# The attention of layer L2: where the softmax is divided by its sums

## Chip, cores and metric

The kernel runs on one core of one Trainium2 chip. The metric is the device time of one execution in microseconds (us); several runs of the same kernel are made, and the median is compared. A profile of one execution says what every engine did and when. The engines are PE (TensorE, matrix products and transposes), DVE (VectorE), ACT (ScalarE), POOL (GpSimd) and SP (which issues transfers). Each works through its own queue in order; they wait for one another by semaphores.

## What is computed

The reference is a network of four layers, each with an attention between two feed-forward halves, on 8 sequences of 512 tokens with 128 features. The change touches the attention of the layer called L2: 16 heads of width 64, causal, with a bias that grows linearly with the distance of the tokens.

```
q, k, v = (x @ Wq), (x @ Wk), (x @ Wv)        # each reshaped to (b, n, 16, 64)
bias    = slope[:, None, None] * (pos[:, None] - pos[None, :])
scores  = einsum('bihd,bjhd->bhij', q, k) * 64 ** -0.5 + bias[None]
scores  = where(pos[:, None] >= pos[None, :], scores, -1e30)
attn    = softmax(scores, axis=-1)
out     = einsum('bhij,bjhd->bihd', attn, v).reshape(b, n, 16 * 64)
return out @ Wo + bo
```

A softmax divides the exponentials of a row by their sum. The division can stand anywhere between the exponential and the end of the product with `v`, since the sum is one number for each head and each query.

## The kernel before

The attention is in `l2_block`. It works in steps `n` = 0 to 63: sequence `b = n // 8`, and in it a pair of heads, so eight steps make a batch (one sequence). A few steps at either end only fill and empty the pipeline. In each step the loop at L1660 writes the work of three neighbouring pairs interleaved:

- `score(n, i)` multiplies the queries of token tile `i` (128 tokens) with all keys up to it (128, 256, 384 or 512 columns), on PE (L1553). One DVE instruction adds the bias and takes the smallest element of each row (L1557), and leaves an ACT exponential to be issued (L1560), which also writes the sums of the rows to `sums[n]`. Signs are turned, so the smallest is what is taken off. Tiles 2 and 1 of pair `n` are scored in step `n`; tiles 3 and 0 already at the end of the step before. The exponentials lie in `es[n]`, 128 x 1280 for each of the two heads.
- `turn(n - 1, m)`, m = 0 to 4, transposes the 128x128 blocks of exponentials of the pair before (L1579, PE), so that keys lie along the partitions; ACT copies each group of four from PSUM (L1581).
- `invert(n - 2)` takes the reciprocals of the sums (L1586, DVE) and spreads each over 64 columns (`rb`, L1588, DVE).
- `weigh(n - 2)` multiplies the turned exponentials with the values into the PSUM tile `o` (L1602, PE). Features lie along its partitions, tokens along its columns. To divide it by the sums, these must be turned too: four transposes of `rb` go to `rp` (L1607, PE), ACT copies `rp` to `rt` (L1609), and DVE multiplies `o` by `rt` into `atts[b]` (L1610).
- `project(n + 1)` makes queries and keys of the next pair (L1522, copied by ACT at L1524), `values(n)` the values of two pairs in every second step (L1535, copied by DVE at L1536), and `leave(b)` once a batch the product with `Wo` (L1616) and the addition to `x` (L1618, DVE).

Between these, three times a step, `works` issues pieces of other layers' work: the feed-forward halves before and after, for sequences that are ready. Their places are written as numbers (`self.plan`): three units to a step. Lines that are named below: L170 statistics for the normalisation and L200 its application on POOL (`whiten`), L310 the products of the last layer's experts (PE's part is L308), L271 and L274 the feed-forward half of L2, L322 to L359 the routing, L906 to L1013 the feed-forward half of L1. The order of PE, ACT and DVE in this stage is that in which the code issues (`manual_schedule`); POOL's and SP's are the scheduler's.

[...] The tile `s` of the scores takes two banks, twice; all else, `tp`, `pp`, `vp`, `o`, `rp`, `op`, `pt`, `yp`, shares four under the tag `mm`. A product can only start when a bank has been read out.

## Time and profile before

| what | value |
|---|---|
| median of 3 runs | 2802.72 us (2797.55 to 2804.87) |
| the profiled execution | 2823.91 us, its span 2822.0 us |
| PE, DVE, ACT, POOL busy | 2508.1, 1886.6, 1741.5, 1177.3 us |
| stage of L2's attention, from its first products to its last | 1143.4 to about 2050 us |
| in it PE, DVE, ACT, POOL busy | 872, 559, 594, 328 us |

The profile comes as a page (busy times, the span in 40 slices, DMA queues, the chain of work that ended last, the costliest groups of instructions) and as a trace that answers questions: what an engine did in a stretch, who waited for whom, what the chain went through. The groups of the lines that the change touches, for the stretch from 1143 to 2052 us (line, engine, operation, tiles, shapes, count | busy us, mean ns | idle time before them):

```profile
L1607 PE MATMUL rp<-cst,rb 128*128 128x128 f32 x256 | 42.0, 286 | 0.2 <-DVE rb L1588 0.2
L1609 ACT COPY rt<-rp 128x512 f32<-128x512 f32 x64 | 37.6, 587 | 142.6 <-PE rp L1607 142.5
L1588 DVE COPY rb<-rc 128x512 f32<-128x512 f32 x64 | 35.7, 557 | 2.2
L1610 DVE TENSOR_TENSOR att<-o,rt 128x512 f32<-128x512 f32 x64 | 44.3, 692 | 161.3 <-ACT rt L1609 161.3
```

A matmul's mean of 286 ns is its time from start to end; four of them in a row overlap.

### The profile page before, as it was taken

What the parts mean: (1) busy time and instruction counts of PE and PEld (TensorE: products, weight loads), DVE (VectorE), ACT (ScalarE), POOL (GpSimd) and SP (SyncE); (2) the same over time, 40 slices, a digit from 0 to 9 for tenths busy, and PEclk for the clock granted to TensorE, in tenths of its full rate; (3) what the DMA queues carried; (4) which work ended last, traced back from release to release, by engine and by line L of the source; (5) the groups of instructions that cost most, each with busy time, mean ns of one, the idle gap of its engine ahead of it and who ended that gap; (6) DMA issues with size and microseconds to landing.
All of it is one profiled execution on the core that took longest, in us unless ns stands there. A gap on an engine that the chain in (4) does not pass through costs nothing.

```text
span 2822.0 us, 51514 instructions
## 1 busy us (share of the span) xinstructions
PE 2508.1 (89%) x18564; PEld 1500.6 (53%) x18564; DVE 1886.6 (67%) x5099; ACT 1741.5 (62%) x4302; POOL 1177.3 (42%) x2073
## 2 busy tenths in 40 slices
PE   5667685799999998899999999999989999999996
PEld 5445453333333343456566656566555666666663
DVE  5235424677777763465666666655589888998897
ACT  2124124166666665676666666666578888988884
POOL 5644356333333442225425344250244454554442
PEclk9877785599999998999999999999999999999998
DMA  8121132000000000000000000000000000000000
GB/s 255 42 68 32 41 89 74 17 17 18 21 19 19 10 18 4 31 1 1 1 1 1 1 1 1 1 1 1 16 9 9 17 20 17 9 17 20 20 2 12
DMA packets 74349, 67.28 MB, mean 24 GB/s; under 512 B 17760, under 2 KB 63848, under 8 KB 71880
## 3 DMA queue, kind: packets, MB, share of 16 engines
q1 hardware_dynamic: 66128, 51.44, 6.8%
q0 software_dynamic: 3872, 8.11, 1.1%
q10 hardware_dynamic: 4096, 4.44, 0.5%
q8 instruction: 148, 2.42, 0.4%
q14 instruction: 105, 0.86, 0.1%
HBM read 36.68 MB, written 27.33 MB: 23 GB/s over the span
## 4 chain that ended last, share of the span: by engine, by line
PE 52%; DVE 16%; ACT 10%; POOL 4%; issue 2%; DMA 0%; SPq 0%; POOLq 0%; ACTq 0%; DVEq 0%
PE tp L1313 7%; PE s L1287 5%; PE s L1130 5%; PE o L1602 4%; PE o L1160 4%; ACT e L1560 4%; PE o L1329 4%; DVE nm L1131 4%; PE s L1553 3%; DVE nm L1291 3%; PE yp L308 3%; PE tp L1579 2%; DVE x L310 2%; PE op L1616 2%; ACT pt L1581 2%
## 5 line engine op out<-in xcount | busy, mean ns | idle before, releaser
L1131 DVE TENSOR_REDUCE nm<-s 128x2 f32<-128x1024 f32 x256 | 305.7, 1218 | 126.7 <-PE s L1150 114.1
L1298 ACT ACTIVATE e<-s,nm 128x512 f32<-128x512 f32 x512 | 344.9, 688 | 26.8 <-DVE nm L1291 22.2
L1152 ACT ACTIVATE pr<-s 128x512 f32<-128x512 f32 x512 | 272.2, 599 | 116.6 <-PE s L1150 106.4
L1319 ACT ACTIVATE p<-tp 128x512 f32<-128x512 f32 x512 | 279.3, 616 | 69.2 <-PE tp L1313 69.2
L1130 PE MATMUL s<-k,q 32*128 32x512 f32 x1024 | 291.4, 676 | 33.6 <-DVE nm L1131 29.2
L1291 DVE TENSOR_REDUCE nm<-s 128x2 f32<-128x1024 f32 x256 | 301.0, 1217 | 27.7 <-PE s L1287 25.8
L1313 PE MATMUL tp<-cst,e 128*128 128x128 f32 x2048 | 293.6, 282 | 24.7 <-DVE rs L1304 14.3
L1313 PEld LDWEIGHTS tp<-cst,e 128*128 128x128 f32 x2048 | 220.4, 142 | 163.0 <-issue 97.8
L1150 PE MATMUL s<-q,k 32*128 32x512 f32 x1024 | 292.1, 639 | 10.4 <-ACT pr L1152 8.6
L1307 POOL TENSOR_SCALAR e<-e,rs 128x512 f32<-128x512 f32 x114 | 199.8, 1753 | 235.5 <-DVE rs L1304 196.0
L1560 ACT ACTIVATE e<-e,m 128x512 f32<-128x512 f32 (+3 forms) x512 | 286.1, 570 | 14.1 <-DVE m L1557 14.0
L1557 DVE CUSTOM_DVE_ANT_0 e<-s,bias 128x512 f32<-128x512 f32 (+3 forms) x512 | 220.1, 486 | 76.6 <-PE s L1553 76.3
L173 POOL TENSOR_TENSOR d<-st 128x4 f32<-128x4 f32 (+2 forms) x97 | 19.8, 204 | 557.1 <-DVE st L170 478.1
L1581 ACT COPY pt<-tp 128x512 f32<-128x512 f32 x320 | 173.8, 590 | 83.4 <-PE tp L1579 83.3
L1307 DVE TENSOR_SCALAR e<-e,rs 128x512 f32<-128x512 f32 x398 | 195.4, 521 | 9.1
L310 DVE SCALAR_TENSOR_TENSOR x<-yp,sel,x 128x128 f32<-128x128 f32 x512 | 178.0, 348 | 31.4 <-PE yp L308 18.8
L1287 PE MATMUL s<-k,q 32*128 32x512 f32 x1024 | 175.1, 648 | 4.8 <-issue 2.5
L1553 PE MATMUL s<-qk 64*128 64x512 f32 (+3 forms) x1024 | 172.7, 456 | 3.1 <-DVE m L1557 2.0
L1579 PE MATMUL tp<-cst,e 128*128 128x128 f32 x1280 | 169.1, 278 | 4.3 <-ACT k L1021 2.6
L1130 PEld LDWEIGHTS s<-k,q 32*128 32x128 f32 x1024 | 88.5, 195 | 153.0 <-DVE nm L1131 102.8
L1329 PE MATMUL o<-p,va 128*32 128x128 f32 x4096 | 165.4, 277 | 2.6 <-ACT p L1319 2.6
L1579 PEld LDWEIGHTS tp<-cst,e 128*128 128x128 f32 x1280 | 139.8, 142 | 39.0 <-issue 14.8
(408 smaller groups left out, 4981.9 us busy)
## 6 DMA issues: line engine op xcount, KB each, us to landing
yd<-z SPq DMA_DIRECT2D x8, 1024.0 KB
r<-yd SPq DMA_DIRECT2D x32, 256.0 KB
xd<-xn SPq DMA_DIRECT2D x16, 256.0 KB
k<-sk SPq DMA_DIRECT2D x64, 64.0 KB
sk<-pu SPq DMA_DIRECT2D x16, 256.0 KB
w<-in_l_w SPq DMA_DIRECT2D x14, 256.0 KB
q<-sq SPq DMA_DIRECT2D x32, 72.0 KB
x<-in_x SPq DMA_DIRECT2D x8, 256.0 KB
```

Source lines behind the costliest of these rows:

```text
L1130: nc.tensor.matmul(s[:, jj, :], lhsT=q[cut, g, i * P : (i + 1) * P], rhs=k[cut, g, :], start=True, stop=True)
L1131: nc.vector.tensor_reduce(nms[b, g // 2][:, i, 2 * h : 2 * h + 2, g % 2], s, AX.X, ALU.max, negate=True)
L1150: nc.tensor.matmul(s, lhsT=k[cut, g, kt * P : (kt + 1) * P], rhs=q[cut, g, :], start=True, stop=True)
L1287: nc.tensor.matmul(s[:, jj, :], lhsT=q[cut, g, i * P : (i + 1) * P], rhs=k[cut, g, :], start=True, stop=True)
L1291: nc.vector.tensor_reduce(nm, scores[n, h], AX.X, ALU.max, negate=True)
L1298: nc.scalar.activation(e, s[:, jj, :], AF.Exp, bias=nm[:, jj : jj + 1], accum_out=sm[:, jj : jj + 1])
L1307: (nc.gpsimd if h and jj and n >= 14 else nc.vector).tensor_scalar(e, e, rc[:, jj : jj + 1], None, ALU.mult)
L1313: nc.tensor.transpose(tp[:, kt, :], probs[n][j][:, kt * P : (kt + 1) * P], self.ident)
L1319: nc.scalar.activation(p, turns[n].pop(0), AF.Exp)
L1329: nc.tensor.matmul(o[32 * j : 32 * j + 32, g * P : (g + 1) * P], lhsT=vas[b % 2][:, kt, 4 * g + j, :], rhs=p2[j][:, kt, :], start=(kt == 0 ...
L1560: outs.append(lambda e=e, jj=jj: nc.scalar.activation(e, e, AF.Exp, bias=mins[n][:, jj, i : i + 1], scale=-1.0, accum_out=sums[n][:, jj, i ...
L1579: nc.tensor.transpose(tp[:, k, :], block(n, jj, i, kt), self.ident)
```

## The change

`invert` and the turned reciprocals are gone: the four transposes, ACT's copy `rt` and DVE's product. In their place `norm` divides the exponentials themselves, ahead of `turn`: for each token tile a reciprocal of two sums a row (one for each head), and two multiplications in place, one for each head, of 128 to 512 columns. It is called twice in a step for the pair `n`: tiles 3 and 0 after the last exponentials of the step are issued, tiles 2 and 1 after `weigh(n - 2)`. ACT copies `o` to `atts[b]`. `turn` and `weigh`'s products are as they were.

```diff
-            def invert(n):
-                rc = wk.tile([P, 2, 4], F32, tag="rc", name="rc")
-                nc.vector.reciprocal(rc, sums.pop(n))
-                rbs[n] = wk.tile([P, 4, 2, 64], F32, tag="rb", name="rb")
-                nc.vector.tensor_copy(rbs[n], bc(rc.rearrange("p j i -> p i j"), 3, 64))
+            def norm(n, *tiles):
+                for i in tiles:
+                    rc = wk.tile([P, 2], F32, tag="rc", name="rc", bufs=4)
+                    nc.vector.reciprocal(rc, sums[n][:, :, i])
+                    for jj in range(2):
+                        e = es[n][:, jj, OFF[i] : OFF[i] + P * (i + 1)]
+                        nc.vector.tensor_scalar(e, e, rc[:, jj : jj + 1], None, ALU.mult)
...
             def weigh(n):
...
-                rp = bank("rp", (P, 4, P))
-                for i in range(4):
-                    nc.tensor.transpose(rp[:, i, :], rb[:, i].rearrange("p j d -> p (j d)"), self.ident)
-                rt = wk.tile([P, 512], F32, tag="rt", name="rt", bufs=1)
-                nc.scalar.copy(rt, rp.rearrange("p i q -> p (i q)"))
-                return lambda: nc.vector.tensor_tensor(atts[b][:, p, :], o, rt, ALU.mult)
+                nc.scalar.copy(atts[b][:, p, :], o)
...
-                    if two:
-                        invert(n - 2)
                     if prev:
                         outs = [turn(n - 1, m) for m in range(3)]
...
                     run(*exps[2:])
+                    if here:
+                        norm(n, 3, 0)
                     works(3 * n)
...
                     if two:
-                        weigh(n - 2)()
+                        weigh(n - 2)
+                    if here:
+                        norm(n, 2, 1)
                     works(3 * n + 1)
```

More of the change, by code (lines that the diff above doesn't have):

```diff
@@ L1512, in bank @@
                 return ps.tile(list(shape), F32, tag="mm", name=name, bufs=4)
-            qs, ks, vs, es, mins, sums, rbs, turned, atts = {}, {}, {}, {}, {}, {}, {}, {}, {}
+            qs, ks, vs, es, mins, sums, turned, atts = {}, {}, {}, {}, {}, {}, {}, {}
             def project(n):
@@ L1581, in turn @@
                 return lambda: nc.scalar.copy(to, tp)
-            def invert(n):
-                rc = wk.tile([P, 2, 4], F32, tag="rc", name="rc")
-                nc.vector.reciprocal(rc, sums.pop(n))
-                rbs[n] = wk.tile([P, 4, 2, 64], F32, tag="rb", name="rb")
-                nc.vector.tensor_copy(rbs[n], bc(rc.rearrange("p j i -> p i j"), 3, 64))
+            def norm(n, *tiles):
[5 more added lines that the diff above has]
+                        nc.vector.tensor_scalar(e, e, rc[:, jj : jj + 1], None, ALU.mult)
             def weigh(n):
-                b, p, t, rb = n // 8, n % 8, turned.pop(n), rbs.pop(n)
+                b, p, t = n // 8, n % 8, turned.pop(n)
                 if p == 0:
```

## The prediction

> **What bounds the kernel now.** I read the page's line of engines and its 40 slices first: they name no single bound, so I looked for the stage that the change touches. Lines 1557 to 1618 run from 1143.4 to about 2050 us. The windows view of that stretch by batch (columns: stretch, length, then busy us and count of PE, PEld, DVE, ACT, POOL, then granted clock and DMA):

> ```profile
> core 0: us, PE busy (x) PEld busy (x) DVE busy (x) ACT busy (x) POOL busy (x), PEclk, DMA share, GB/s
> 1385.00:1500.00 115.00, 110.60 (x671) 69.49 (x670) 73.58 (x277) 75.30 (x210) 46.83 (x110) 1.00 0.00 1
> 1500.00:1616.00 116.00, 111.59 (x675) 70.42 (x674) 74.58 (x282) 76.29 (x214) 47.83 (x110) 1.00 0.00 1
> ```

> PE is at work for 112 of 116 us at full clock, with no DMA; DVE and ACT have a third free. But busy is no proof of a bound, so I followed the chain of waits through one batch, 1500 to 1560 us (start, length, what):

> ```profile
> 1536.25 1.99 PE vp L1535 x8
> 1538.24 2.30 PE o L1602 x16
> 1540.55 0.59 PE rp L1607 x4
> 1541.13 0.89 PE op L271 x8
> 1542.03 1.28 PE s L1553 x8
> 1543.31 1.46 PE tp L1579 x12
> 1544.77 1.72 PE pp L1522 x4
> 1546.49 1.28 PE s L1553 x8
> 1547.76 1.02 PE tp L1579 x8
> 1548.79 2.30 PE o L1602 x16
> ```

> A step (one pair of heads) goes round on PE alone here, and the four transposes `rp` stand in its chain. Elsewhere in the batch some 6 to 8 us of a step go through ACT (copies `pt` and exponentials), and then come back to PE; `rp` is in the chain there too, since it stands ahead of the turn that feeds ACT. So all 64 `rp` count.

> **What goes.** PE: 64 x 0.59 us = 37.8 us, all of it on the chain. ACT: the copy `rt`, 64 x 586 ns. DVE: reciprocal 194 ns, copy `rb` 557 ns (median 428), product `att` 692 ns: 1.44 us a step. A wait goes with it; from the view of waits for the stage (us in total, times, longest), and from the page's groups what is to price the new work:

> ```profile
> DVE att L1610 <- ACT rt L1609: 161.3, 63, 5.8
> L1307 DVE TENSOR_SCALAR e<-e,rs 128x512 f32<-128x512 f32 x398 | 195.4, 521 | 9.1
> L1307 POOL TENSOR_SCALAR e<-e,rs 128x512 f32<-128x512 f32 x114 | 199.8, 1753 | 235.5 <-DVE rs L1304 196.0
> ```

> DVE stood 2.6 us a step behind `rt`, holding back the next scores' reductions (L1557). Those may now start earlier.

> **What comes.** ACT: a copy of `o`, 128x512 from PSUM, 64 x 586 ns by the row of `rt`: it cancels the copy that goes, and stands in the same place of ACT's queue, so I cost it at nothing. DVE: per step four reciprocals 128x2 at 158 ns (row of L1304) and eight multiplies, two each of 128, 256, 384 and 512 columns. The same instruction exists in the attention of the last layer, L3 (L1307): median 486 ns at 512 columns. At 4 columns with a scalar operand L1013 takes 230 ns. The line between gives 292, 357, 421, 486 ns, eight of them 3.11 us; with reciprocals 3.74 us busy. Start to start it is less; the timeline of DVE (start, length):

> ```profile
> 2062.76 0.15 DVE L1304 RECIPROCAL rs<-sm 128x2 f32<-128x2 f32 x1
> 2062.94 0.91 DVE L1307 TENSOR_SCALAR e<-e,rs 128x512 f32<-128x512 f32 x2
> 2063.77 0.16 DVE L1304 RECIPROCAL rs<-sm 128x2 f32<-128x2 f32 x1
> ```

> One tile of 512 takes 1.01 us, so 0.88, 0.75, 0.62 for the shorter: 3.26 us a step, in two calls of about 1.63 us (tiles 3 and 0; tiles 2 and 1). DVE gains 2.3 us busy a step, 147 us in all; it was busy 559 of the stage's 906.6 us, and would be busy about 79%. As a total, it fits.

> [...]

> **The new wait.** A turn (L1579) waited for the exponentials on ACT; now it waits for DVE to finish `norm(n, 2, 1)`, which in DVE's queue stands behind the reductions, `norm(n, 3, 0)`, the planned work of that third of the step, the copies `v` (L1536), and once a batch the product behind `leave` (L1618). Behind it wait the next planned work and the reductions L1557, for which ACT's exponentials and PE's next scores wait. I set the finish of `norm(n, 2, 1)` against the time at which PE, 0.59 us earlier, would start the turn, for the eight steps from 1507 us; all other durations are those of before.

> - Hidden: step with `o` at 1538.24. The copies `v` end at 1538.97, the call at 1540.6; PE is there at 1543.31 - 0.59 = 1542.7. To spare 2.1.
> - Just late: `o` at 1548.79. Reductions end at 1548.9 (0.55 earlier, as reciprocal and `rb` no longer stand ahead), + 1.63 + statistics 0.78 + L959 to L962 1.10 + 1.63 = 1554.1; due 1553.84. Late 0.2.
> - Late: `o` at 1573.60. Reductions end 1573.71, + 1.63 + routing (L351 to L329) 1.66 + 1.07 + 1.63 = 1579.7; due 1577.27: 2.4 late. ACT had waited for DVE there already, and the step loses 1.9; of this 0.9 comes back two steps on, where PE waited for L1021 behind DVE.
> - The others have 3.1, 4.1, 2.0, 4.3 and 0.4 to spare; the step with `leave` has 3.1 although the product holds the call until PE is through.

> A batch gains 8 x 0.59 = 4.7, loses 0.2 and 1.9, gets back 0.9, and 0.4 where the `rb` of 1611.26 had taken 1.55 us: 3.9.

> [...] The row L1307 with GpSimd multiplying beside it shows 521 against 486: 0.3 a step; the row `rb` of this stage 557 against 428: 1.0. I take 0.7, and as most steps have room, 0.7 a batch on the path: 3.2 a batch remain. [...]

> **Ends of the stage.** In the first batch GpSimd's whitening already holds PE (`pt` waits for `xn` at 1181), and its statistics now stand behind a 1.63 us call; the first three steps are waits for exponentials, + about 1 us each; small losses besides: 4.7 - 1.65 - 3 - 1.5 = -1.5. From 1848 to 1952: two tight steps lose 0.5 and 1.6, together with small ones 2.5: +2.2. In the last batch PE waits for `xn` at 1980 to 1986, again 1.65 later, and the last turn, ready with the exponential at 2028, comes about 2 later: +0.5. The norms at these ends are estimates from the same rows, 0 to 2 us each.

> **Sum.** 5 x 3.2 - 1.5 + 2.2 + 0.5 = 17 us. The profiled execution took 2823.9 us (span 2822.0); it would take 2807. The median of the runs, 2802.7, would go to 2786 with the same difference.

> **Rivals.**
> 1. DVE's call, not PE's time, sets the step (slower). Place: before each turn. For it: in three of eight steps the room is under half a microsecond, and `rb` once took 1.55 us beside GpSimd. Against: the same multiply beside GpSimd is 7% longer on average. If a call takes 1.6 times as long (2.6 us), the finish comes 2 us later: 2.0, 2.0 and 1.6 more are lost in those three steps, so a batch loses 1.7, five 8, the ends 8: 2820. It decides from about 1.4 times on, where the gain is gone. Chance 0.32.
> 2. All of PE's time is won, since reductions that start earlier repay the late steps: 2802.7 - 37.8 = 2765. For it the 161 us of DVE's wait that goes; against it the 2.4 us late turn. Chance 0.12.
> 3. Time off PE turns into waits for DVE, equal in size: 2803. Chance 0.12.
> 4. That the transposes stay is excluded: PE's order in the changed program has none.

> The forecast has 0.44, its own range 2772 to 2795. About 0.3% (8 us) is what a measurement of this kernel can tell from no change. Faster by more: 0.42 of the forecast, rival 2: 0.54; same: 0.13; slower: 0.33. The range for 8 in 10 reaches to both sides, 2763 to 2822.

> **What would show it.** Right: `rp` and `rt` gone; PE busy in the stage 38 us less; multiplies near 486 ns at 512 columns; waits "tp <- DVE" few and in steps with routing work or statistics ahead of the call; PE's share of a middle batch near 107 of 113 us. Wrong: multiplies far over 500 ns, or a wait of the turn for DVE in most steps, or reductions that ACT's exponentials wait for.

## The result and the profile after

The changed kernel takes 2789.9 us (median, 2786.6 to 2795.4) against 2802.7 for the kernel before: ratio 0.9954, 95% interval 0.9944 to 0.9965. When both were timed again later, the ratio was 0.9965 (0.9951 to 0.9979). So 10 to 13 us were won where 17 were forecast. The profiled execution took 2792.7 us, its span 2790.8.

From the page after, the line of engines (busy us, share of the span, instructions), and from the groups by line and shape, 1120 to 2052 us, those of the new instructions:

```profile
PE 2474.8 (89%) x18308; PEld 1470.4 (53%) x18308; DVE 2015.8 (72%) x5675; ACT 1743.7 (62%) x4302; POOL 1195.4 (43%) x2073
```

```profile
L1590 DVE TENSOR_SCALAR e<-e,rc 128x512 f32<-128x512 f32 x128 | 63.6, 539 | 2.3
...
L1590 DVE TENSOR_SCALAR e<-e,rc 128x384 f32<-128x384 f32 x128 | 50.7, 438 | 2.3
...
L1590 DVE TENSOR_SCALAR e<-e,rc 128x256 f32<-128x256 f32 x128 | 41.7, 367 | 2.3
L1587 DVE RECIPROCAL rc<-sm 128x2 f32<-128x2 f32 x256 | 40.5, 158 | 1.5 <-ACT e L1560 1.5
L1590 DVE TENSOR_SCALAR e<-e,rc 128x128 f32<-128x128 f32 x128 | 33.2, 313 | 2.3
```

Over the program PE lost 33 us of busy time and DVE gained 129; ACT kept its own. But PE's total in two profiles of the kernel before differs by 12 us (2508.1 and 2495.8), so the stage alone is the better measure, from its first scores to the last `leave` (before, then after):

```profile
1147.45:2041.69 894.24, 860.01 (x5184) 539.79 (x5185) 555.30 (x2067) 593.13 (x1656) 326.78 (x744) 1.00 0.01 2
1120.81:2006.93 886.12, 836.69 (x4928) 517.32 (x4929) 682.90 (x2644) 594.21 (x1656) 341.95 (x744) 0.99 0.01 2
```

PE is busy 23 us less there, where the prediction named 38 as a sign, and DVE 128 us more. (The columns are length, then busy us and count of PE, PEld, DVE, ACT and POOL, then granted clock, DMA share and GB/s.) The eight multiplies of a step take 2 x (539 + 438 + 367 + 313) = 3.31 us.

The stage by batch, in the windows view that was shown of before (two middle batches of the changed kernel):

```profile
core 0: us, PE busy (x) PEld busy (x) DVE busy (x) ACT busy (x) POOL busy (x), PEclk, DMA share, GB/s
1474.37:1587.25 112.88, 107.47 (x643) 66.91 (x642) 90.33 (x352) 76.00 (x212) 49.80 (x110) 1.00 0.00 1
1587.25:1700.13 112.88, 107.45 (x643) 66.90 (x642) 90.39 (x352) 75.99 (x212) 49.62 (x110) 1.00 0.00 1
```

PE is busy 107.5 of 112.9 us, DVE 80%. Before, PE was busy 111.3 of 115.7. Three waits of the whole stage (us in total, times, longest):

```profile
ACT att L1607 <- PE o L1604: 115.9, 41, 9.3
...
PE tp L1579 <- DVE e L1590: 19.0, 13, 2.4
...
PE pt L237 <- POOL xn L200: 8.8, 10, 4.3
```

ACT's long wait for `o` takes the place of that for `rp` (142.5 us before); no engine's wait in the trace ends with the copy of `o`, so it costs PE nothing. `pt`'s wait for GpSimd isn't new: it was 5.4 us before. The turn's wait for the division is new, 19 us in 13 waits. In a middle batch it comes once. The timeline of PE there (start, length, what, and in brackets the idle time before it):

```profile
1547.21 1.35 PE L1553 MATMUL s<-qk 64*128 64x512 f32 x8
1548.49 0.33 PE L1579 MATMUL tp<-cst,e 128*128 128x128 f32 x1
1550.67 1.42 PE L1579 MATMUL tp<-cst,e 128*128 128x128 f32 x11 [1.85 <-DVE e L1590]
```

And the timeline of DVE about it:

```profile
1543.34 0.56 DVE L1557 CUSTOM_DVE_ANT_0 e<-s,bias 128x384 f32<-128x384 f32 x1 [1.89 <-PE s L1553]
...
1546.57 0.18 DVE L351 TENSOR_REDUCE ls<-pr 128x4 f32<-128x32 f32 x1
...
1548.12 0.19 DVE L329 TENSOR_TENSOR bt1o<-bt1r,bt1f 128x32 f32<-128x32 f32 x1
...
1550.26 0.62 DVE L1590 TENSOR_SCALAR e<-e,rc 128x256 f32<-128x256 f32 x2
...
1563.04 1.51 DVE L310 SCALAR_TENSOR_TENSOR x<-yp,sel,x 128x128 f32<-128x128 f32 x4 [1.16 <-PE yp L308]
```

Between the two brackets DVE's timeline shows no other: from 1543.3 to 1561.9 us it works without a gap. The routing (L351 to L329) stands in this stretch, ahead of the second call, and the second call ends at 1550.9. That is the step that the prediction named.

The lengths of the eight batches tell where the time went. They are read off PE's timeline, from the stage's first scores (L1553) to the first `leave` product, then from one `leave` to the next; the last column is the rest, which is the last layer, L3. The rows "again" are second profiles, told below.

| kernel | 1st | 2nd | 3rd | 4th | 5th | 6th | 7th | 8th | stage | L3 |
|---|---|---|---|---|---|---|---|---|---|---|
| before | 123.3 | 114.0 | 115.7 | 115.7 | 115.7 | 116.7 | 104.1 | 89.1 | 894.2 | 780.3 |
| before, again | 123.2 | 114.0 | 115.7 | 115.7 | 116.6 | 115.1 | 104.1 | 89.6 | 893.9 | 780.5 |
| after | 128.2 | 112.3 | 112.9 | 112.9 | 112.9 | 112.9 | 102.3 | 91.7 | 886.1 | 783.9 |
| after, again | 127.2 | 113.7 | 112.9 | 112.9 | 112.9 | 113.3 | 102.4 | 89.8 | 884.9 | 785.1 |

Some batches differ between two profiles of one kernel. There the granted clock differs: it is 0.98 to 0.99 instead of 1.00 in the sixth batch of before, the fifth of before again and the second and sixth of after again; in the first batch it is 1.00 before and 0.97 after, and in the last 0.94 to 0.98 in all four.

A middle batch at full clock wins 2.8 us. The first loses 4 to 5, the last 0.2 to 2.6; the stage as a whole wins 8 to 9 us, and L3, which the change does not touch, takes 3.4 to 4.8 more. Stage and L3 together win 4.5 us, in either pair of profiles.

### The profile page after: what moved, and what is told of

Its sections match the earlier page's. It is cut to its first block, busy times and chain, and to the rows that moved or that the text cites. A ratio compares the mean times of both kernels' runs of the same rounds, so it can differ in the third digit from the quotient of the medians.

```text
span 2790.8 us, 51558 instructions
## 1 busy us (share of the span) xinstructions
PE 2474.8 (89%) x18308; PEld 1470.4 (53%) x18308; DVE 2015.8 (72%) x5675; ACT 1743.7 (62%) x4302; POOL 1195.4 (43%) x2073
## 4 chain that ended last, share of the span: by engine, by line
PE 54%; DVE 17%; ACT 6%; POOL 5%; issue 2%; DMA 1%; SPq 0%; POOLq 0%; ACTq 0%; DVEq 0%
PE tp L1313 8%; PE s L1287 6%; PE s L1130 5%; PE o L1160 4%; PE o L1329 4%; PE o L1604 4%; DVE nm L1131 4%; PE s L1553 4%; PE yp L308 3%; PE tp L1579 3%; DVE nm L1291 3%; PE pp L1522 3%; ACT e L1560 2%; PE s L1150 2%; PE op L1613 2%
## 5 line engine op out<-in xcount | busy, mean ns | idle before, releaser
L1131 DVE TENSOR_REDUCE nm<-s 128x2 f32<-128x1024 f32 x256 | 305.7, 1218 | 126.2 <-PE s L1150 113.7
L1152 ACT ACTIVATE pr<-s 128x512 f32<-128x512 f32 x512 | 272.3, 598 | 116.7 <-PE s L1150 106.7
L1291 DVE TENSOR_REDUCE nm<-s 128x2 f32<-128x1024 f32 x256 | 301.0, 1217 | 30.2 <-PE s L1287 28.6
L1313 PE MATMUL tp<-cst,e 128*128 128x128 f32 x2048 | 294.5, 282 | 24.5 <-DVE rs L1304 14.5
L1307 POOL TENSOR_SCALAR e<-e,rs 128x512 f32<-128x512 f32 x114 | 199.9, 1753 | 238.6 <-DVE rs L1304 202.7
L1557 DVE CUSTOM_DVE_ANT_0 e<-s,bias 128x512 f32<-128x512 f32 (+3 forms) x512 | 220.1, 486 | 109.0 <-PE s L1553 108.9
L310 DVE SCALAR_TENSOR_TENSOR x<-yp,sel,x 128x128 f32<-128x128 f32 x512 | 178.1, 348 | 43.5 <-PE yp L308 30.8
L1307 DVE TENSOR_SCALAR e<-e,rs 128x512 f32<-128x512 f32 x398 | 195.9, 522 | 9.3 <-DVE rs L1304 0.2
L1590 DVE TENSOR_SCALAR e<-e,rc 128x512 f32<-128x512 f32 (+3 forms) x512 | 189.1, 414 | 9.1
L1579 PE MATMUL tp<-cst,e 128*128 128x128 f32 x1280 | 174.2, 281 | 21.4 <-DVE e L1590 19.0
L1553 PE MATMUL s<-qk 64*128 64x512 f32 (+3 forms) x1024 | 173.8, 458 | 1.8 <-ACT qk L1524 1.2
L1579 PEld LDWEIGHTS tp<-cst,e 128*128 128x128 f32 x1280 | 142.7, 143 | 58.2 <-DVE e L1590 21.4
```

Source lines behind the costliest of these rows:

```text
L1131: nc.vector.tensor_reduce(nms[b, g // 2][:, i, 2 * h : 2 * h + 2, g % 2], s, AX.X, ALU.max, negate=True)
L1291: nc.vector.tensor_reduce(nm, scores[n, h], AX.X, ALU.max, negate=True)
L1307: (nc.gpsimd if h and jj and n >= 14 else nc.vector).tensor_scalar(e, e, rc[:, jj : jj + 1], None, ALU.mult)
L1313: nc.tensor.transpose(tp[:, kt, :], probs[n][j][:, kt * P : (kt + 1) * P], self.ident)
L1553: nc.tensor.matmul(s[:, jj, 0:w], lhsT=qs[n][cut, i * P : (i + 1) * P], rhs=ks[n][cut, 0:w], start=True, stop=True)
L1579: nc.tensor.transpose(tp[:, k, :], block(n, jj, i, kt), self.ident)
```

## The experiments

The theory is that a step goes round on PE, so that 4.7 us a batch go with `rp`, and that DVE takes some back at the places where its queue is full (A). Its main rival: DVE is the bound in general, and what it does is paid for in every step.

### Before, once more

The profiled execution of before reached the stage at 1147.4 us, that of the changed kernel at 1120.8. The change touches nothing ahead of the stage.

> The kernel before, profiled once more, because in the two profiles at hand the stage of L2's attention begins 26.7 us apart (first scores at 1147.45 and 1120.8 us), with no difference in the code ahead of it. If that is how executions differ, this profile has first scores anywhere from 1115 to 1150 us, and the stage itself (first scores to the last leave's products) again takes 894.4 us within 1 us, a middle batch 115.7. If the change did it (placement of tiles), first scores come at 1147 again.

It took 2798.5 us, reached the stage at 1122.3 and needed 893.9 us for it (before: 894.2). So the 26 us ahead of the stage differ between two executions of one kernel, and the stage repeats to 0.3 us. Batches can be compared between single executions where their granted clock is the same; spans can't.

### No division at all

```diff
-                    if here:
-                        norm(n, 3, 0)
...
-                    if here:
-                        norm(n, 2, 1)
```

This leaves out the division by the sums, and so gives all that the change takes away and nothing that it adds.

> The changed kernel without any division by the sums (both calls of norm left out; the exponentials go on undivided). Theory A (PE's time sets the stage, and only a late turn takes some back): the whole of PE's saving shows, 64 x 0.59 = 37.8 us off the kernel before, 2765, and a middle batch takes 115.7 - 4.7 = 111.0. Theory B (PE's time given back to ACT's copies and exponentials anyway): hardly under the changed kernel, 2782 to 2790, a middle batch above 112.

2761.6 us (ratio 0.9853, 0.9831 to 0.9874); the stage takes 853.4. The windows view of a middle batch (columns as above):

```profile
1459.42:1569.20 109.78, 106.71 (x642) 66.91 (x641) 64.70 (x256) 75.75 (x212) 47.50 (x110) 1.00 0.00 1
```

A batch falls from 115.7 to 109.8: 5.9, more than the 4.7 of `rp`. PE is busy 4.6 us less than before (111.3 to 106.7) and idle 1.3 less (4.4 to 3.1). `rp` and the DVE work of `rb`, the reciprocal and the product went together here, so this run can't say what the transposes gave alone; the next one can. Against the changed kernel, the 25.6 us of DVE work that the divisions add to a batch (90.3 less 64.7) cost 112.9 - 109.8 = 3.1 us: 12% of it. In the first batch the difference is 128.2 - 114.9 = 13.4, of which some 2.5 to 3.5 are the clock (below, "The ends").

### The transposes put back

```diff
+                rp = bank("rp", (P, 4, P))
+                for i in range(4):
+                    nc.tensor.transpose(rp[:, i, :], wq[:, 2, i * P : (i + 1) * P], self.ident)
                 nc.scalar.copy(atts[b][:, p, :], o)
```

Four transposes of a weight tile that is always there, into a bank that nobody reads: PE's work of before with DVE's work of after.

> The changed kernel with four transposes a step put back on PE at their old place (of a constant tile, read by nobody). Theory A: they are on the chain in every step but the one where the turn waits for DVE anyway: 7 x 0.59 = 4.1 us a middle batch, 112.9 to 117.0, and about 33 us in all, 2823, slower than the kernel before. Theory B: transposes hide behind ACT in half of the steps: 2805 or less.

2814.4 us (ratio 1.0042, 1.0027 to 1.0056). Middle batches took 115.7, 2.8 more than without, where theory A asked for 4.1. The wait view, middle batches:

```profile
PE tp L1579 <- DVE e L1590: 5.1, 4, 1.3
```

The turn waits 1.3 us a batch instead of 1.85: PE is later, and part of its added time goes into the wait. PE is busy 110.9 us of the batch instead of 107.5, so the transposes add 3.4 us and not 4.7, and its idle time falls by 0.6. The direction is A's, the size about 60% of it.

These batches are as long as those of before, 115.7, although DVE is busy 89.9 us in them and was busy 74.3. So in a middle batch all that the change wins is the transposes, 2.8 us, and its other half, more work on DVE against the wait for `rt`, comes out even.

### The second call moved ahead of the planned work

```diff
-                        norm(n, 3, 0)
+                        norm(n, 3, 0, 2, 1)
...
-                    if here:
-                        norm(n, 2, 1)
```

> The changed kernel with the second call of norm joined to the first, ahead of the planned work of the step's first third, so that routing (L351 to L329), L959 to L962, statistics and the copies v no longer stand before it in DVE's queue. Theory A: the turn that waited 1.85 us a batch no longer does, 112.9 to about 111.2 a batch and 10 us in all, 2780. Rival: DVE now stands still until ACT has made the last exponentials, and what is behind it (statistics, products of the experts, copies v, and with them banks) comes late: 2795 or more.

2818.5 us (ratio 1.0057, 1.0035 to 1.0078): slower than both kernels. Waits in three middle batches (1366 to 1720 us):

```profile
ACT e L1560 <- DVE m L1557: 12.1, 6, 3.4
DVE rc L1587 <- ACT e L1560: 11.7, 23, 1.0
PE s L1553 <- DVE m L1557: 7.7, 3, 2.6
```

At that place the exponentials of tiles 2 and 1 are not done, so DVE stops for them 23 times; the reductions behind it come late, ACT waits for these, and once a batch PE's scores wait 2.6 us for a bank. In these batches (116.5 us) the granted clock is 0.97, which is part of the loss. My expectation failed: I had looked at when the turn needs the division, not at when its input is ready.

A smaller move, tile 2 alone ahead of the planned work (`norm(n, 3, 0, 2)`, then `norm(n, 1)`):

> The changed kernel with the division of tile 2 (0.75 us) issued with tiles 3 and 0, ahead of the planned work, and only tile 1 left for the second call. The run with all four tiles early lost 29 us, as the early call stood behind exponentials that were not yet done, and what stood behind it (statistics, reductions) came late. Theory A (the loss there comes from waiting for the last exponentials, those of tiles 2 and 1, of which tile 2's are the earlier ones): with only tile 2 moved the loss is less than half: middle batches 113 to 115, median 2790 to 2805. Rival (the exponentials of tile 2 are done when the early call ends, so nothing waits, and the turn comes 0.75 us earlier): middle batches 112.2, median about 2785.

2791.7 us (ratio 0.9971, 0.9961 to 0.9982). Middle batches 112.6, near the rival's 112.2, and the median in the range of theory A: nothing is won over the changed kernel. The second batch took 114.4, but there the clock was 0.985, as in the second batch of the changed kernel's second profile (113.7).

### The routing moved by a third of a step

```diff
-... (n + 6, n + 10, n + 11, n + 12, n + 14, *range(n + 16, n + 24)), *self.l3_ffn_steps(b, w3, bank))
+... (n + 6, n + 10, n + 11, n + 13, n + 14, *range(n + 16, n + 24)), *self.l3_ffn_steps(b, w3, bank))
```

> The changed kernel with one piece of planned work moved by a third of a step: the routing's second part (L351 to L329, 1.66 us of VectorE, once a batch) is issued behind the second call of the divisions instead of ahead of it. Theory A (a turn that waits for VectorE behind routing work is what one step of each middle batch loses): the 1.85 us wait of the turn for VectorE at that place goes; a middle batch falls from 112.9 to about 111.2 us, five of them and the ones beside them give 8 to 11 us: median about 2780. Rival (VectorE is the bound of that step in any order, so what stands behind the call is late in its turn: reductions, exponentials, next scores): middle batches stay at 112.4 to 113, the wait turns up as scores or exponentials that wait for reductions, median 2787 to 2791.

2789.5 us (ratio 0.9965, 0.9954 to 0.9977), middle batches 112.9 as before the move: theory A's 111.2 failed. PE's timeline at the same place:

```profile
1551.78 1.42 PE L1579 MATMUL tp<-cst,e 128*128 128x128 f32 x11 [0.30 <-DVE e L1590]
1553.04 1.88 PE L1522 MATMUL pp<-xta,wqkv 128*128 128x512 f32 x4
1556.38 1.35 PE L1553 MATMUL s<-qk 64*128 64x384 f32 x8 [1.46 <-DVE m L1557]
```

The turn now waits 0.30 us instead of 1.85, and the next scores wait 1.46 for the reductions, which stand behind the routing in its new place. The time only changed its name. So theory A had the right place and the wrong cause: it isn't the order of two pieces within the step. What I took from it, theory B: DVE has no gap over 18.6 us, so it is the bound in that stretch, in any order, and only work taken out of it gains.

### The routing moved by a whole step

```diff
-... (n + 6, n + 10, n + 11, n + 12, n + 14, *range(n + 16, n + 24)), *self.l3_ffn_steps(b, w3, bank))
+... (n + 6, n + 10, n + 11, n + 16, n + 17, *range(n + 18, n + 26)), *self.l3_ffn_steps(b, w3, bank))
```

> The changed kernel with the routing's second and third parts (3.2 us of VectorE a batch, L351 to L302) a whole step later, and the experts' products (L308, L310) two thirds of a step later. In the changed kernel VectorE works without a gap from 1543.3 to 1562.0 in a middle batch (18.7 us, and the late turn lies in it); moving the second part by a third of a step kept all in that stretch and gained nothing in a middle batch. Theory B (VectorE is the bound over that stretch, and only work taken out of it gains): middle batches fall from 112.9 to 110.7 to 111.5 us, six of them and the neighbours 8 to 13 us, median 2777 to 2782. Rival 1 (the next step, with 1.2 and 1.8 us free, fills up and is late in its turn): middle batches 112.5 to 113.5, median 2787 to 2793. Rival 2 (what is lost is not VectorE's time at all, but PE's chain through ScalarE's copies): nothing changes either, but VectorE then shows gaps in that stretch while the batch stays at 112.9.

The edit moves two things: the routing's second and third parts by a step or more, and the experts' products behind it (L308, L310) by two thirds of a step. They were not moved singly. 2782.5 us (ratio 0.9952, 0.9933 to 0.997), half a microsecond above B's range; the stage takes 870.6, 15.6 less than in the changed kernel. Of these, 2.6 lie in the first batch, in which nothing was moved, and are the clock; the last batch gives 3.8, also at a higher clock (0.98 for 0.94). The wait of the turn in the middle batches, and three batches in the windows view (columns as above, the last three PEclk, DMA share and GB/s):

```profile
PE tp L1579 <- DVE e L1590: 1.2, 4, 0.3
```

```profile
1357.46:1469.95 112.49, 109.28 (x641) 67.69 (x640) 90.54 (x352) 75.84 (x212) 49.38 (x111) 0.98 0.00 1
1469.95:1582.45 112.50, 109.29 (x642) 67.62 (x641) 90.74 (x352) 75.86 (x212) 49.71 (x111) 0.98 0.00 1
1582.45:1693.54 111.09, 107.64 (x641) 66.96 (x640) 91.03 (x352) 75.85 (x212) 49.62 (x111) 1.00 0.00 1
```

At full clock a batch takes 111.1, inside theory B's 110.7 to 111.5, with 0.3 us of waiting at the turn and the same work on DVE. But two of the batches took 1.4 us more with the clock at 0.98, and this decides how much is seen of it (more in the last section).

The number is B's, its reason is not. In the third of these batches DVE still works without a gap, and for longer than before: from 1667.7 to 1697.9, 30.2 us, between these two brackets of its timeline:

```profile
1667.68 0.69 DVE L1536 COPY v<-vp 128x512 f32<-128x512 f32 x1 [0.96 <-PE vp L1535]
...
1700.88 0.69 DVE L1615 TENSOR_TENSOR x<-x,op 128x512 f32<-128x512 f32 x1 [3.02 <-PE op L1613]
```

In this stretch PE waits once, and for ACT:

```profile
1674.69 1.98 PE L1522 MATMUL pp<-xta,wqkv 128*128 128x512 f32 x4 [0.44 <-ACT k L1021]
```

So a stretch without a gap is no proof that DVE holds PE up. What the runs show is narrower: in its old step the routing makes the turn late (1.85 us), a third of a step later the turn and the scores (0.30 and 1.46), and in the next step nothing that PE waits for.

> The changed kernel itself once more, so that it and the kernel with the routing a step later are timed beside each other. Middle batches 112.9 us, except where the granted clock falls to a half for about 3.4 us, which adds about 1.5 us to a batch and need not come in the same batch as in the first profile. Median 2784 to 2792, ratio to the kernel before 0.995 to 0.997.

> The kernel with the routing a step later, timed beside the changed kernel. Theory B (15 us less in the stage, of which the last layer keeps some 3 back through the granted clock): 6 to 13 us less than the run beside it, ratio to the kernel before 0.991 to 0.995; middle batches 111.1, or 112.5 where the clock falls. Rival (the stage of the first profile was a lucky one): within 3 us of the run beside it.

Timed beside each other, the changed kernel took 2789.0 us (ratio 0.9965, 0.9951 to 0.9979) and this one 2781.7 (0.9934, 0.9917 to 0.9952): 7.3 us less, within the 6 to 13 that were expected. This time all four middle batches had the low clock (112.5), and still the stage took 873.7 against 884.9; most of the 11.2 us lie in the second batch (4.6) and in the first (which is the clock), the seventh and the last (1.5 to 1.8 each), only 0.3 to 0.7 in each middle one. It is the best version found, and beats both kernels.

### Each multiply twice

```diff
                         nc.vector.tensor_scalar(e, e, rc[:, jj : jj + 1], None, ALU.mult)
+                        nc.vector.tensor_scalar(e, e, 1.0, None, ALU.mult)
```

> The changed kernel with every division multiplied once more by 1.0 in place, eight more VectorE multiplies a step (128 to 512 columns, together 3.3 us by the durations of the profile, so each call takes twice as long). It prices the rival that the call on VectorE sets the step. Theory A (one step in eight has no room, most have 2 to 4 us): the second call ends 3.3 us later in each step; with the rooms of 2.0, 3.1, 3.1, 4.1, 4.3, 0.4, 0 and 0 us that the prediction worked out, a middle batch loses 1.3 + 0.2 + 0.2 + 2.9 + 3.3 + 3.3 = 11 us at most, and about 7 if the calls overlap their neighbours: 120 to 124 us a batch, median 2840 to 2880. Rival (VectorE is already the bound, at 79% busy with its order fixed): all 3.3 us of each step are added, 139 us a batch, median near 3000.

2915.4 us (ratio 1.0414, 1.0395 to 1.0432), middle batches 128.4 to 129.9. A batch, and the waits of the middle batches:

```profile
1524.17:1654.02 129.85, 114.74 (x641) 70.64 (x640) 109.58 (x416) 76.47 (x212) 51.42 (x110) 0.95 0.00 1
```

```profile
PE tp L1579 <- DVE e L1591: 32.6, 12, 4.7
```

Between the two expectations, and both rested on too large an addition: DVE gained 109.4 - 90.4 = 19 us a batch, not 26. For these, 15.5 to 17 us were paid, 80 to 90%, a part of it through the clock (0.95 in this batch). Beside the run without division, where 12% were paid, three points make a bend: up to some 80% busy DVE's work was nearly free in the middle batches, beyond it most was paid. Where between the points the bend lies they don't tell. The rival is right past it, and not at the size of the change.

### One reciprocal a call

```diff
+                lo, hi = min(tiles), max(tiles)
+                rc = wk.tile([P, 2, 2], F32, tag="rc", name="rc", bufs=4)
+                nc.vector.reciprocal(rc, sums[n][:, :, lo : hi + 1 : hi - lo])
```

> The changed kernel with one reciprocal of 128x2x2 a call instead of two of 128x2: two VectorE instructions of 158 ns fewer a step, the same numbers. Each call is about 0.15 us shorter. Theory A (only the one late turn of each batch is paid for by VectorE): 0.15 to 0.3 us a batch, 1 to 3 us in all, median 2787 to 2790, hardly to be told from none. Rival (VectorE's time counts in every step): 0.3 us x 64 = 19 us, median about 2771.

2789.1 us (ratio 0.9956, 0.9939 to 0.9973), middle batches 112.5: 0.4 us better, a little over theory A's 0.15 to 0.3 and far from the rival's 2.4. Together with the routing a step later:

> The same with one reciprocal of 128x2x2 a call. By itself the single reciprocal took 0.4 us off a middle batch (112.9 to 112.5) and nothing that the time shows. Theory B (it counted only inside the stretch in which VectorE is the bound): with that stretch relieved it is worth 0 to 0.2 us a batch, median within 3 us of the run beside it. Rival (short instructions count everywhere): 0.4 us a batch again and more at the ends, 3 to 5 us less than the run beside it.

2790.9 us (ratio 0.9979, 0.9969 to 0.999): 8 us worse than the routing alone, so both expectations failed. Waits in three middle batches:

```profile
DVE rc L1587 <- ACT e L1560: 3.2, 3, 1.1
PE tp L1579 <- DVE e L1591: 2.9, 3, 1.0
```

The single reciprocal has to wait for the later of its two tiles. While DVE was behind, the exponentials were long done; now that it isn't, it stops 1.1 us a batch for them and the turn 1.0 after it. At the same clock this costs 0.4 to 0.5 us a batch (111.6 against 111.1 at 1.00, 112.9 against 112.5 at 0.98). The larger part of the loss is elsewhere: the stage takes 880.1 against 870.6, and of these 9.5 us the first and the last batch have 6.3, at a lower clock than there (0.97 for 0.99, and 0.93 for 0.98). Whether the single reciprocal brought the lower clock is open.

## Why the prediction was nearly right

The median was forecast at 2786 and came at 2789.9. Its steps:

- **What goes: right in kind, too large.** The transposes did lie on PE's path: put back, they made a middle batch 2.8 us longer. But 0.59 us is what they take from end to end. In the trace of before the next product starts 0.52 us after the first of them (mean of 64), since products overlap, and PE's busy time fell by 3.8 us a middle batch, not 4.7. The copy of `o` cost nothing.
- **Durations: right, a little low.** 313, 367, 438 and 539 ns where 292, 357, 421 and 486 were taken. The excess is 2 x (21 + 10 + 17 + 53) ns, 0.2 us a step. If GpSimd's neighbourhood made all of it, that is less than the 0.7 taken, which was my estimate between two rows, and near the 0.3 of the row L1307. DVE's busy time rose by 129 us where 147 were written. Single multiplies reach 1.7 us.
- **The late turn: right in place and size.** The step with the routing waits 1.85 us, 1.9 was written. That it lay in the order ahead of the call was wrong: with the routing behind the call the scores wait instead. The other step, 0.2 late, was not late. Of the 0.9 us that were to come back where PE waits for L1021, 0.1 came (a wait of 0.41 for 0.52); the 0.4 behind `rb` did come.
- **The middle: right, with two errors that cancel in part.** 2.8 us a batch won for 3.2, and PE busy 107.5 of 112.9 for "107 of 113". The sum was 4.7 off PE less 1.5 of new waits; it became 3.8 less 1.0 (PE's idle time went from 4.4 to 5.4).
- **The ends: the waits were larger, the batch was not; the clock was left out.** The first batch was put at -1.5 and took -4.0 to -5.0. Its waits in the changed kernel:

```profile
PE tp L1579 <- DVE e L1590: 5.4, 5, 2.1
PE pt L237 <- POOL xn L200: 2.2, 4, 0.7
```

The turn waits five times for 5.4 us, where the prediction had 1 us for each of three steps; DVE, which also makes the bias tiles in this batch, was busy 79.4 us of it before and 102.2 after. Yet the run with the routing a third of a step later does the same work in this batch, waits 5.5 us in five times at the turn, and took 124.7; that with the routing a whole step later took 125.6. So the work costs 1.4 to 2.3 us, near the forecast. Most of the rest is the clock. The first products of the stage, in the changed kernel and in the run with the routing a third later:

```profile
1120.81 2.50 PE L1553 MATMUL s<-qk 64*128 64x512 f32 x8 [0.69 <-ACT qk L1524]
...
1125.48 1.35 PE L1553 MATMUL s<-qk 64*128 64x512 f32 x8 [0.69 <-ACT qk L1524]
```

In both profiles of the changed kernel a stretch at half clock lasts 5 us into the stage; in both of the kernel before it ends just ahead of it. The seventh batch was put at +2.2 and gave 1.7 to 1.8. The last was put at +0.5 and took -0.2 to -2.6: its final turn waited 2.4 us, as "about 2" said, and its clock was 0.94 and 0.96.

- **The rest of the program: left out, and luck.** 17 us were forecast for the stage; it gave 8 to 9, and L3 took about 4 back, so both together gave 4.5. The medians differ by 10 to 13 all the same. The other 5 to 8 us lie ahead of the stage, where the change does nothing, and why is not settled: the changed kernel reached the stage at 1120.8 and 1114.6 us, the kernel before at 1147.4 and 1122.3, the other versions at 1113.9 to 1125.8, and only two executions of each were profiled. That the median came within 4 us of the forecast is in part luck.

Of the rivals, the call that sets the step is real but needs more work on DVE than the change brings, as the run that multiplies twice shows; the full saving is the kernel without division. The equal trade is closest to what happens at the two ends.

## What to carry to other kernels

Ask not how busy the receiving engine is on average, but which of its instructions another engine waits for, and how much room each has in the order in which they stand. A stretch without a gap does not answer that: 18.6 us without a gap held a late turn here, 30.2 us in the next version held none. When a wait is found, moving work to just behind it can merely rename the wait; move it to a step in which everything behind it has room, and compare the stage, not the wait. Look at the filling and draining batches by themselves, and compare batches only at the same granted clock: here the clock took as much of the first batch as the change did, or more.

## What the hardware did unexpectedly

In the kernel with the routing a step later the granted clock of PE fell to a half after two waits of 0.69 and 0.60 us. In half microseconds (columns as in the windows view):

```profile
1393.50:1394.00 0.50, 0.00 (x0) 0.00 (x0) 0.17 (x1) 0.50 (x2) 0.25 (x2) 1.00 0.00 0
1394.00:1394.50 0.50, 0.49 (x2) 0.47 (x3) 0.00 (x0) 0.50 (x2) 0.50 (x4) 1.00 0.00 0
1394.50:1395.00 0.50, 0.50 (x3) 0.42 (x3) 0.00 (x0) 0.50 (x3) 0.42 (x3) 0.72 0.00 0
1395.00:1395.50 0.50, 0.50 (x2) 0.41 (x2) 0.04 (x1) 0.50 (x3) 0.34 (x3) 0.50 0.00 0
...
1398.00:1398.50 0.50, 0.50 (x6) 0.21 (x4) 0.50 (x2) 0.00 (x0) 0.50 (x1) 0.86 0.00 0
1398.50:1399.00 0.50, 0.50 (x6) 0.26 (x4) 0.46 (x3) 0.00 (x0) 0.50 (x2) 1.00 0.00 0
```

Worked out from the 0.72 and 0.86, the half clock lasts from about 1394.7 to 1398.1: 3.4 us. It costs 1.4 us a batch (112.5 for 111.1). In the third batch of the same run the same two waits stand before the same products, and the clock stays. The changed kernel's late turn (1.85 us idle) kept the clock; in its first batch, 2.12 us were followed by 0.50, and the turn took 2.61 us instead of 1.42:

```profile
1143.04 2.61 PE L1579 MATMUL tp<-cst,e 128*128 128x128 f32 x11 [2.12 <-DVE e L1590]
```

In L3 both profiles of before have one such fall beyond those at its beginning and end; the changed kernel's two have three and four. A fall cost up to 1.4 us in the batches above; two or three more could be 3 to 4 us, about what L3 took longer: 3.6 and 4.8. The other runs agree in the main. The three profiles with one such fall have L3 at 780.3, 780.5 and 781.3 us, and the last of these is the run with the routing a third of a step later, which divides as the changed kernel does; the other eleven have three or four, and 782.9 to 787.2 us there, the run without any division among them. So the division alone doesn't bring the falls; whether the place of PE's waits on the grid does was not tried.
